# Four graph layers on one core: turning blocks by VectorE and DMAs in the second layer, and on two queues for the fourth

## The chip, the core and the metric

The kernel runs on one core of a Trainium2 chip, in one launch. Its time is the device time of the program in microseconds, from executions on the chip. A core has TensorE (PE in the profile), VectorE (DVE), ScalarE (ACT), GpSimd (POOL) and SyncE (SP). SP does no arithmetic and only issues DMAs; POOL computes and issues DMAs too. A queue is the order in which one engine issues its DMAs. Sixteen DMA engines carry them all.

## The reference

There are 4096 nodes with 256 features each and one 0/1 adjacency matrix. Four graph layers follow each other, and each ends in `x = layernorm(x + layer(x))`.

```python
# layer 0: additive attention, 4 heads, leaky_relu 0.2, masked softmax over j, elu
e = leaky_relu(s_i[:, None, :] + s_j[None, :, :], 0.2);  alpha = softmax(where(adj, e, -inf), axis=1)
# layer 1: dot-product attention, 4 heads of 64
q = x @ Wq + bq;  k = x @ Wk + bk;  v = x @ Wv + bv        # each split into 4 heads
scores = einsum('hnd,hmd->hnm', q, k) / 8 + (edge.T - 1) * 10000
ctx = einsum('hnm,hmd->hnd', softmax(scores), v)
# layer 2: additive attention, one head, slope 0.01, elu
# layer 3: cosine attention on features of width 128
att = softmax(where(adj > 0, normalise(x @ Wk.T) @ normalise(x @ Wq.T).T, NEG), axis=1)
out = 0.5 * (att @ x) + 0.5 * x
```

The text counts the layers from one: the second layer is the dot-product attention, the fourth is the cosine attention.

## The kernel before

All of it is float32. The features stay on the chip in `X`, 128 partitions by 32 tiles of 128 rows. A block is four tiles, 512 rows, so there are eight blocks (`NB = 8`, `QB = 4`, `QW = 512`). Every layer makes attention weights for one block of queries against one tile of keys at a time (a unit), always with the keys on the partitions, so that the product with the values needs no transpose of the weights. The weights of a unit are made on ScalarE (the exponential or a relu) and VectorE (the product with the mask), and TensorE sums over the keys into PSUM. The order of TensorE's work is written out by hand (`tc.manual_schedule`); in the second layer's attention those of VectorE and ScalarE are too. For the rest the framework's scheduler decides, and it moves an instruction ahead when it holds its inputs and its buffers to be there. Every engine issues in order, so an instruction that waits holds up what stands behind it on its engine or queue.

A projection of a block needs that block turned, with the features on the partitions. Two helpers do it. `transposed_block` (L112) lets TensorE do eight transposes of 128 x 128 (L118) into two PSUM banks, and two copies bring them to SBUF (L120). `turned_apart` (L123, called through `block_apart`, L138) does without TensorE: VectorE transposes 32 x 32 squares inside each quarter of the partitions (L130, two instructions of 128 x 512), one DMA writes the 512 KB result `squares` to DRAM (L133), and four DMAs of 128 KB read it back with the quarters exchanged (L135). The rows of the block come out in another order this way.

The second layer (`multi_head_attention`, L531) starts with a prologue. For each block TensorE turns it (`turn`, L564), multiplies it by Wk and Wq (`keys`, L567, matmuls L572, then ScalarE adds the bias at L576 and VectorE takes the largest magnitude at L577), and by Wv (`values`, L580, matmuls L587, additions L592 from two PSUM buffers `pv`). In the loop at L618 a pass turns block b, takes the values of block b - 1 and the keys of block b; block 0 was turned in the first layer. Then come 8 blocks of 64 half tiles of 64 keys: `scores` (L634) loads the mask, multiplies k and q of all four heads (L645) and lets ScalarE take the exponential (L647); `weights` (L649) multiplies by the mask on VectorE (L657) and adds up the row sums, on POOL (L664) for even half tiles and by an accumulating DMA from POOL's queue (L670) for odd ones, the first two of a block by plain DMAs from SP (L668); `sums` (L672) multiplies by V (L678). The weights `prob` have eight buffers. The mask is in bytes: during the first layer `narrow` (L946) copies the matrix from int32 to bytes in DRAM, in pieces `edges` of 64 rows by 16 half tiles by 512 columns, and `narrow_edges` gives four half tiles of one piece, so that each of two DMAs (L640) moves 64 partitions of 2 KB.

The third layer (`additive_one`, L401) has 8 blocks of 32 units: `weights` (L444: relu on ScalarE, L451; the mask on VectorE, L453) and `sums` (L455, four matmuls L459). The mask comes in int32 from SP, 512 KB for two units, into four buffers. During its last block the fourth layer is prepared by `Cosine.prepare` (L837), for blocks 0 to 5: step 0 turns X with `block_apart`; step 1 projects the block onto 128 features for queries and 128 for keys on TensorE (L852) and scales them to unit length as `rows`; step 2 turns `rows` with `turned_apart` into `T`. The calls stand at L513 and L521; one block follows another every four units, and step 1 stands eight units behind step 0. Both turnings go through POOL's queue, one buffer `squares` (pool `co_once`) and two in DRAM (`co_dram`). Blocks 6 and 7 are prepared in the fourth layer's first block, with both turnings on SP's queue. POOL's queue also carries the fourth layer's masks (L835), some of them behind a small copy that holds them back (`behind`, L91).

The fourth layer (`cosine_attention`, L868) has 8 blocks of 32 units again, with matmuls of `T` against `T` (L889) and of the weights against `X` (L901).

Of the kernel before, what the change touches and what calls it, by code (L numbers as in the profile page):

```python
# [9 lines left out]
FP = mybir.dt.float32  # L10
# [8 lines left out]
P = 128  # L19
# [9 lines left out]
def kernel(  # L29
# [92 lines left out]

    def turned_apart(once, dr, part, to, eng):  # L123

        B = P // QB
        squares = once.tile([P, QB, KC, P], FP, name="squares")
        for c in range(KC):
            nc.vector.transpose(squares[:, :, c, :].rearrange("p q (k n) -> p k q n", n=B),  # L130
                                part(c).rearrange("p k (q f) -> p k q f", f=B))
        far = dr.tile([QB, B, QB, KC * P], FP, name="squares_far")
        eng.dma_start(far.rearrange("a f q m -> (a f) (q m)"), squares.rearrange("p q c m -> p (q c m)"))  # L133
        for q in range(QB):
            eng.dma_start(to[q * B:(q + 1) * B], far[:, :, q, :].rearrange("a f m -> f a m"))  # L135
        return to.rearrange("p a (c m) -> p c a m", c=KC)
# [264 lines left out]
    def additive_one(w_sb, slope, tail, op, follow):  # L401
# [3 lines left out]
        with ExitStack() as lay:  # L405
# [18 lines left out]
            def turn(b):  # L424
                return transposed_block(sb, bank, b)

# [104 lines left out]
    def multi_head_attention(w_sb, b_sb, tail, rows_of_den, narrow_edges):  # L531
# [12 lines left out]
        with ExitStack() as lay:  # L544
# [7 lines left out]
            with ExitStack() as pro:  # L552
                wp = pool(pro, "mh_w", 1)
                sb = pool(pro, "mh_in", 3)
                ps = pool(pro, "mh_ps", 6, space=PSUM)
# [11 lines left out]
                def keys(b):  # L567
                    for n, to, scale in (("k", kT, 1.0), ("q", qT, qscale)):
                        for o in range(KC):
                            pk = bank()  # L570
                            for c in range(KC):
                                nc.tensor.matmul(pk, w_sb[n][:, c, o * P:(o + 1) * P],  # L572
                                                 xTs[b][:, c].rearrange("p k i -> p (k i)"),
                                                 start=(c == 0), stop=(c == KC - 1))
                            part = to[:, o, b * QW:(b + 1) * QW]
                            nc.scalar.activation(part, pk, AF.Identity, bias=b_sb[n][:, o:o + 1], scale=scale)  # L576
                            nc.vector.tensor_reduce(big[n][:, b, o:o + 1], part, AX.X, OP.max,  # L577
                                                    apply_absolute_value=True)

                def values(b):  # L580


                    for k in range(0, QB, KC):
                        pv = pv2.tile([P, KC, D], FP, name="pv")
                        for s in range(KC):
                            for c in range(KC):
                                nc.tensor.matmul(pv[:, s, :], xTs[b][:, c, k + s], w_sb["v"][:, c, :],  # L587
                                                 start=(c == 0), stop=(c == KC - 1))
                        j = 2 * (b * QB + k)
                        for n in range(2):  # L590
                            for r in range(2):
                                nc.vector.tensor_tensor(V[r * d:(r + 1) * d, j + n:j + n + 2 * KC - 1:2, :],  # L592
                                                        pv[n * d:(n + 1) * d, :, r * P:(r + 1) * P],
                                                        b_sb["v"][n * d:(n + 1) * d, r * P:(r + 1) * P].unsqueeze(1)
                                                        .to_broadcast([d, KC, P]), OP.add)
# [213 lines left out]
    class Cosine:  # L809
# [7 lines left out]
        def start(self):  # L817
# [5 lines left out]
            self.T = [keep.tile([P, QB, 2 * P], FP, name=f"T{b}") for b in range(NB)]  # L823
            self.dram = self.stack.enter_context(tc.tile_pool(name="co_dram", bufs=2, space=bass.MemoryType.DRAM))
            self.once = self.stack.enter_context(tc.tile_pool(name="co_once", bufs=1, side="right", reuse_waits="tile"))
            self.w_sb = keep.tile([P, KC, 2 * P], FP, name="w3_sb")
            load_w(self.w_sb[:, :, :P], wq3T, nc.sync)
# [116 lines left out]
    todo = iter([(b, j) for b in range(NB) for j in range(0, 2 * NT, NJ)])  # L944

    def narrow(z):  # L946

        for b, j in itertools.islice(todo, 1):
            slim_edges[b, j] = slim.tile([P // 2, NJ, QW], U8, name=f"edges{b}_{j}")
            with behind(z):  # L950
                nc.gpsimd.dma_start(slim_edges[b, j],
                                    adj.rearrange("(t p) i -> p t i", p=P // 2)[:, j:j + NJ, b * QW:(b + 1) * QW])

    def narrow_edges(b, j, n):
        return slim_edges[b, j - j % NJ][:, j % NJ:j % NJ + n, :]

# [70 lines left out]
```

## Time and profile before

| | |
|---|---|
| time | 2911.56 us, median of 3 runs (2909.53 to 2911.84) |
| profiled execution | 2912.43 us; 2910.7 us of it from first to last instruction |
| mean granted clock of TensorE | 0.997 |

| stretch, us from the start | what | PE busy, us | DVE | ACT | POOL | DMA share |
|---|---|---|---|---|---|---|
| 0 to 724 | first layer | 720.3 | 667.2 | 661.4 | 63.1 | 0.65 |
| 724 to 816 | second layer, prologue | 91.5 | 57.2 | 31.7 | 0.0 | 0.00 |
| 816 to 1717 | second layer, attention | 900.2 | 686.8 | 566.6 | 807.3 | 0.89 |
| 1717 to 2232 | third layer | 506.3 | 300.6 | 226.0 | 49.9 | 0.58 |
| 2232 to 2911 | fourth layer | 671.1 | 242.4 | 169.6 | 44.9 | 0.39 |

Busy time is the time in which an engine had an instruction at work. The DMA share is the mean busy share of the 16 DMA engines. PEld is TensorE's load of the stationary operand, which runs beside its matmuls. In the lines of the profile a group is named by its line in the kernel, its engine, its operation and `output<-input` in the program's names.

### The profile page before, as it was taken

Reading aid. Unit: us, or ns where it says so; the run is one execution under the profiler, and the core shown is the slowest. Engines: PE = TensorE matmul, PEld = TensorE weight load, DVE = VectorE, ACT = ScalarE, POOL = GpSimd, SP = SyncE. Lnnn points to the kernel's source line nnn. Section 1 sums busy time; section 2 is a strip of 40 time slices with the busy share of each in tenths; the row PEclk is TensorE's granted clock in tenths of the full one; section 3 lists DMA queues with packets and bytes.
Section 4 is the critical chain, followed back from the end, with each engine's and each line's share of the span. In section 5 each row is a group of like instructions: output and inputs, shape, how many; then the busy total and the mean of one; then the engine's idle time right before and its main releaser. Section 6 shows DMA issues by size and latency. Waiting matters only on the chain.

```text
span 2910.7 us, 50256 instructions
## 1 busy us (share of the span) xinstructions
PE 2889.4 (99%) x20141; PEld 1553.4 (53%) x20141; DVE 1954.2 (67%) x2541; ACT 1655.3 (57%) x2589; POOL 965.2 (33%) x735
## 2 busy tenths in 40 slices
PE   9999999999999999999999999999998999999998
PEld 4333333333643333333333358888887777777776
DVE  8899999998677777777777765655666423333333
ACT  7899999997356666666666654444443222222222
POOL 0010010100068989989889860000012000000000
PEclk9999999999999999999999999999999999999999
DMA  7566667665068989889889875655566434434341
GB/s 205 103 138 137 139 139 145 135 129 90 1 134 193 185 186 193 183 187 192 182 189 191 182 171 133 178 163 150 154 185 168 87 58 58 58 58 58 58 58 29
DMA packets 214061, 391.72 MB, mean 135 GB/s; under 512 B 16338, under 2 KB 94146, under 8 KB 212931
## 3 DMA queue, kind: packets, MB, share of 16 engines
q0 software_dynamic: 106336, 190.35, 40.2%
q1 hardware_dynamic: 107216, 197.88, 22.3%
q8 instruction: 158, 2.59, 0.3%
q14 instruction: 77, 0.62, 0.1%
q10 hardware_dynamic: 274, 0.26, 0.0%
HBM read 325.46 MB, written 29.43 MB: 122 GB/s over the span
## 4 chain that ended last, share of the span: by engine, by line
PE 98%; DMA 1%; DVE 1%; ACT 0%; issue 0%; POOL 0%; DVEq 0%; POOLq 0%
PE acc L293 23%; PE acc L901 15%; PE acc L678 15%; PE p L645 15%; PE acc L459 8%; PE g L459 7%; PE p L889 4%; PE g L889 3%; PE g L572 2%; PE g L196 1%; PE pv L587 1%; PE acc L196 1%; PE g L118 1%; PE acc L852 1%; DMA squares_far<-squares 1%; PE g L305 0%
## 5 line engine op out<-in xcount | busy, mean ns | idle before, releaser
L657 DVE TENSOR_TENSOR prob<-p,mask 128x1024 f32<-128x1024 f32 x512 | 624.1, 1223 | 209.5 <-ACT p L647 203.8
L647 ACT ACTIVATE p<-p,shift 128x1024 f32<-128x1024 f32 x512 | 556.2, 1088 | 325.2 <-PE p L645 324.4
L293 PE MATMUL acc<-prob,V 128*32 128x512 f32 x6144 | 664.0, 592 | 1.2 <-DVE prob L283 1.2
L664 POOL TENSOR_TENSOR den<-den,prob 128x1024 f32<-128x1024 f32 x248 | 626.9, 2528 | 72.6 <-DVE prob L657 64.7
L280 ACT ACTIVATE prob<-row,dst 128x512 f32<-128x512 f32 x1020 | 633.1, 712 | 0.1
L283 DVE SCALAR_TENSOR_TENSOR prob<-prob,mask 128x2048 f32<-128x2048 f32 x256 | 582.5, 2286 | 24.2 <-ACT prob L280 20.7
L645 PE MATMUL p<-qT,kT 64*64 64x512 f32 x4096 | 532.3, 590 | 0.8 <-DVE prob L657 0.8
L678 PE MATMUL acc<-prob,V 64*64 64x512 f32 x4096 | 531.5, 589 | 0.0
L901 PE MATMUL acc<-X,prob 128*128 128x257 f32 x2048 | 485.5, 380 | 0.0
L901 PEld LDWEIGHTS acc<-X,prob 128*128 128x128 f32 x2048 | 388.6, 190 | 162.8 <-issue 112.9
L894 DVE TENSOR_TENSOR prob<-prob,mask 128x512 f32<-128x512 f32 x256 | 176.2, 690 | 409.3 <-ACT prob L893 408.1
L293 PEld LDWEIGHTS acc<-prob,V 128*32 128x32 f32 x6144 | 197.3, 110 | 453.1 <-issue 433.6
L451 ACT ACTIVATE e<-row,dst 128x512 f32<-128x512 f32 x256 | 184.0, 721 | 241.8 <-DVE prob L453 212.6
L678 PEld LDWEIGHTS acc<-prob,V 64*64 64x64 f32 x4096 | 155.9, 133 | 285.4 <-issue 278.1
L645 PEld LDWEIGHTS p<-qT,kT 64*64 64x64 f32 x4096 | 154.4, 133 | 277.3 <-issue 261.5
L453 DVE SCALAR_TENSOR_TENSOR prob<-e,mask 128x512 f32<-128x512 f32 x256 | 177.6, 695 | 173.4 <-PE acc L459 93.9
L91 POOL COPY tick<-prob 128x1 f32<-128x1 f32 x35 | 40.0, 1144 | 645.9 <-DVE prob L283 644.8
L835 POOL DMA_DIRECT2D mask<-in_adjT x64 | 47.6, 743 | 582.2 <-DVE prob L894 505.3
L670 POOL DMA_DIRECT2D den<-prob x240 | 231.6, 965 | 14.7 <-DVE prob L657 7.5
L893 ACT ACTIVATE prob<-p 128x512 f32<-128x512 f32 x144 | 85.7, 596 | 257.0 <-PE p L889 243.0
L459 PE MATMUL acc<-V,prob 128*128 128x257 f32 x1024 | 225.1, 380 | 0.0
L459 PE MATMUL g<-V,prob 128*128 128x257 f32 x1024 | 224.1, 380 | 0.0
(160 smaller groups left out, 1965.6 us busy)
## 6 DMA issues: line engine op xcount, KB each, us to landing
mask<-in_adjT SPq DMA_DIRECT2D x256, 512.0 KB
den<-prob POOLq DMA_DIRECT2D x240, 512.0 KB, 5.3
mask<-edges SPq DMA_DIRECT2D x256, 128.0 KB
mask<-in_adjT POOLq DMA_DIRECT2D x64, 512.0 KB, 5.7
edges<-in_adj POOLq DMA_DIRECT2D x32, 512.0 KB, 10.0
den<-prob SPq DMA_DIRECT2D x16, 512.0 KB
row<-far SPq DMA_DIRECT2D x7, 1024.0 KB
squares_far<-squares POOLq DMA_DIRECT2D x12, 512.0 KB, 4.0
```

The source lines that it names most:

```text
L280: nc.scalar.activation(z[:, h, :], r, AF.Relu, bias=-1.0, scale=dst[:, j, h:h + 1])
L283: nc.vector.scalar_tensor_tensor(z, z, 1.0, mask[m][:, j % MJ, :].unsqueeze(1).to_broadcast([P, H, QW]), OP.add, OP.mult)
L293: nc.tensor.matmul(acc[b][h * G:(h + 1) * G, n, :], part, prob[b, j][:, h, :], start=(j == 0), stop=(j == NT - 1))
L459: nc.tensor.matmul(acc[b][k][:, :D + 1], prob[b, j][:, k * P:(k + 1) * P], V[:, j, :], start=(j == 0), stop=(j == NT - 1))
L645: nc.tensor.matmul(p[c * d:(c + 1) * d, r, :], kT[half, c, j * d:(j + 1) * d], qT[half, c, cols], start=True, stop=True)
L647: nc.scalar.activation(p, p, AF.Exp, bias=shift)
L657: nc.vector.tensor_tensor(z, p, mask[m][:, j % MJ, :].unsqueeze(1).to_broadcast([P, KC, QW]), OP.mult)
L664: nc.gpsimd.tensor_tensor(to, to, flat, OP.add)
L670: nc.gpsimd.dma_start(to, flat, accum_op=OP.add)
L678: nc.tensor.matmul(acc[b][c][r * d:(r + 1) * d, :], V[half, j, r * d:(r + 1) * d], prob[b, j][half, r, :], start=(j == 0), stop=(j == NH - 1))
L889: nc.tensor.matmul(p.rearrange("p (k i) -> p k i", k=QB), T[j // QB][:, 0, j % QB], T[b][:, 1], start=True, stop=True)
L901: nc.tensor.matmul(acc[b][k], prob[b, j][:, k * P:(k + 1) * P], X[:, j, :], start=(j == 0), stop=(j == NT - 1))
```

## The change

In the second layer, blocks 2 to 7 are turned by `block_apart` on SP's queue, one pass of the loop ahead of their use, with four xT buffers instead of three; block 1 is still turned by TensorE. The keys of these blocks then stand in the order in which the turning leaves them. The queries are put back in order as ScalarE writes them (L587 of the changed kernel), V is stored by the new order (L603), `scores` takes the keys from a column `at`, and the bytes of the mask are kept in pieces of 32 rows by 32 quarter tiles, from which four DMAs of 32 partitions fetch a mask tile, for the first 16 half tiles of a block in runs of 512 bytes. For the fourth layer step 0 has its own buffers (`follow.turning`: three xT buffers, which the third layer's own turnings use first, one `squares`, and DRAM) and goes to SP's queue; step 2 stays on POOL's for blocks 0 to 5. `rows` moves to the pool with one buffer.

```diff
-    def turned_apart(once, dr, part, to, eng):
+    def turned_apart(squares, far, part, to, eng):
-        squares = once.tile([P, QB, KC, P], FP, name="squares")
+        squares = squares.tile([P, QB, KC, P], FP, name="squares")
+        far = far.tile([QB, B, QB, KC * P], FP, name="far")
...
-        far = dr.tile([QB, B, QB, KC * P], FP, name="squares_far")
@@ additive_one
+            xp = pool(lay, "gb_turn", 3)
+            sq = pool(lay, "gb_squares", 1)
+            far = pool(lay, "gb_far", 2, space=bass.MemoryType.DRAM)
+            follow.turning = xp, sq, far
...
-                return transposed_block(sb, bank, b)
+                return transposed_block(xp, bank, b)
@@ multi_head_attention
-                sb = pool(pro, "mh_in", 3)
+                sb = pool(pro, "mh_in", 4)
+                sq = pool(pro, "mh_sq", 1)
+                dr = pool(pro, "mh_far", 2, space=bass.MemoryType.DRAM)
...
-                                nc.tensor.matmul(pk, w_sb[n][:, c, o * P:(o + 1) * P],
-                                                 xTs[b][:, c].rearrange("p k i -> p (k i)"),
+                                nc.tensor.matmul(pk.rearrange("p (k i) -> p k i", k=QB),
+                                                 w_sb[n][:, c, o * P:(o + 1) * P], xTs[b][:, c],
...
+                            if n == "q" and b > 1:
+                                part, pk = (t.rearrange(how, a=QB, n=P // QB) for t, how in
+                                            ((part, "p (k a n) -> p a k n"), (pk, "p (a k n) -> p a k n")))
...
+                    turn(1)
                     for b in range(1, NB):
-                        turn(b)
+                        if b < NB - 1:
+                            xTs[b + 1] = block_apart(sb, sq, dr, b + 1, nc.sync)
...
                     for c in range(KC):
-                        nc.sync.dma_start(mask[m][c * d:(c + 1) * d], narrow_edges(b, j, MJ))
+                        for s in range(2):
+                            lo = c * d + s * d // 2
+                            nc.sync.dma_start(mask[m][lo:lo + d // 2], narrow_edges(b, j, s))
...
+                at = j * d if j < 4 * QB else j // (2 * QB) * QW + j % QB * P + j % (2 * QB) // QB * d
...
-                        nc.tensor.matmul(p[c * d:(c + 1) * d, r, :], kT[half, c, j * d:(j + 1) * d], qT[half, c, cols],
+                        nc.tensor.matmul(p[c * d:(c + 1) * d, r, :], kT[half, c, at:at + d], qT[half, c, cols],
@@ Cosine.prepare
-            eng = nc.gpsimd if b < NB - 2 else nc.sync
             if step == 0:
-                self.xT[b] = block_apart(in_, self.once, self.dram, b, eng)
+                self.xT[b] = block_apart(*self.turning, b, nc.sync)
...
-                rows = self.rows[b] = in_.tile([P, QB, 2, P], FP, name="rows")
+                rows = self.rows[b] = self.once.tile([P, QB, 2, P], FP, name="rows")
...
-                turned_apart(self.once, self.dram, lambda n: rows[:, :, n, :], self.T[b], eng)
+                turned_apart(self.once, self.far, lambda n: rows[:, :, n, :], self.T[b],
+                             nc.gpsimd if b < NB - 2 else nc.sync)
@@ cosine_attention
+            co.turning = (pool(lay, "co_turn", 2), pool(lay, "co_squares", 1),
+                          pool(lay, "co_turn_far", 2, space=bass.MemoryType.DRAM))
@@ narrow, narrow_edges
-    NJ = 16
+    NJ = 32
...
-            slim_edges[b, j] = slim.tile([P // 2, NJ, QW], U8, name=f"edges{b}_{j}")
+            slim_edges[b, j] = slim.tile([P // QB, NJ, QW], U8, name=f"edges{b}_{j}")
...
-    def narrow_edges(b, j, n):
-        return slim_edges[b, j - j % NJ][:, j % NJ:j % NJ + n, :]
+    def narrow_edges(b, j, s):
+        t = 2 * j
+        part = slim_edges[b, t - t % NJ]
+        if j < 4 * QB:
+            return part[:, t + s:t + s + 2 * QB - 1:2, :]
+        t = t % NJ // (QB * QB) * QB * QB + (j % (2 * QB) // QB * 2 + s) * QB
+        return part[:, t:t + QB, :]
```

More of the change, by code (lines that the diff above doesn't have):

```diff
@@ L571, in keys @@
                             for c in range(KC):
[L572 to L573 removed]
+                                nc.tensor.matmul(pk.rearrange("p (k i) -> p k i", k=QB),
+                                                 w_sb[n][:, c, o * P:(o + 1) * P], xTs[b][:, c],
                                                  start=(c == 0), stop=(c == KC - 1))
                             part = to[:, o, b * QW:(b + 1) * QW]
+                            if n == "q" and b > 1:
+                                part, pk = (t.rearrange(how, a=QB, n=P // QB) for t, how in
+                                            ((part, "p (k a n) -> p a k n"), (pk, "p (a k n) -> p a k n")))
                             nc.scalar.activation(part, pk, AF.Identity, bias=b_sb[n][:, o:o + 1], scale=scale)
[L577 removed]
+                            nc.vector.tensor_reduce(big[n][:, b, o:o + 1], to[:, o, b * QW:(b + 1) * QW], AX.X, OP.max,
                                                     apply_absolute_value=True)
@@ L588, in values @@
                                                  start=(c == 0), stop=(c == KC - 1))
-                        j = 2 * (b * QB + k)
                         for n in range(2):
+                            j = slice(None, KC) if b > 1 else slice(None, 2 * KC - 1, 2)
+                            first = 2 * b * QB + (n * QB + k if b > 1 else 2 * k + n)
+                            j = slice(first, first + j.stop, j.step)
                             for r in range(2):
-                                nc.vector.tensor_tensor(V[r * d:(r + 1) * d, j + n:j + n + 2 * KC - 1:2, :],
+                                nc.vector.tensor_tensor(V[r * d:(r + 1) * d, j, :],
                                                         pv[n * d:(n + 1) * d, :, r * P:(r + 1) * P],
@@ L823, in start @@
             self.T = [keep.tile([P, QB, 2 * P], FP, name=f"T{b}") for b in range(NB)]
-            self.dram = self.stack.enter_context(tc.tile_pool(name="co_dram", bufs=2, space=bass.MemoryType.DRAM))
             self.once = self.stack.enter_context(tc.tile_pool(name="co_once", bufs=1, side="right", reuse_waits="tile"))
+            self.far = self.stack.enter_context(tc.tile_pool(name="co_far", bufs=2, space=bass.MemoryType.DRAM))
             self.w_sb = keep.tile([P, KC, 2 * P], FP, name="w3_sb")
@@ L938, in cosine_attention @@
                         outputs(b, QB if b < NB - 1 else 2)
-    NJ = 16
+    NJ = 32
     slim = ctx.enter_context(tc.tile_pool(name="slim", bufs=1, space=bass.MemoryType.DRAM))
     slim_edges = {}
-    todo = iter([(b, j) for b in range(NB) for j in range(0, 2 * NT, NJ)])
+    todo = iter([(b, j) for b in range(NB) for j in range(0, QB * NT, NJ)])
     def narrow(z):
         for b, j in itertools.islice(todo, 1):
-            slim_edges[b, j] = slim.tile([P // 2, NJ, QW], U8, name=f"edges{b}_{j}")
+            slim_edges[b, j] = slim.tile([P // QB, NJ, QW], U8, name=f"edges{b}_{j}")
             with behind(z):
                 nc.gpsimd.dma_start(slim_edges[b, j],
-                                    adj.rearrange("(t p) i -> p t i", p=P // 2)[:, j:j + NJ, b * QW:(b + 1) * QW])
-    def narrow_edges(b, j, n):
-        return slim_edges[b, j - j % NJ][:, j % NJ:j % NJ + n, :]
+                                    adj.rearrange("(t p) i -> p t i", p=P // QB)[:, j:j + NJ, b * QW:(b + 1) * QW])
+    def narrow_edges(b, j, s):
[5 more added lines that the diff above has]
+        return part[:, t:t + QB, :]
     w2_sb = const.tile([P, KC, D + 2], FP, name="w2_sb")
```

## The prediction

> **What bounds the kernel now.** I read the page first, then PE's waits, then the places they name.
>
> ```profile
> PE 2889.4 (99%) x20141; PEld 1553.4 (53%) x20141; DVE 1954.2 (67%) x2541; ACT 1655.3 (57%) x2589; POOL 965.2 (33%) x735
> ...
> PE 98%; DMA 1%; DVE 1%; ACT 0%; issue 0%; POOL 0%; DVEq 0%; POOLq 0%
> ```
>
> TensorE is the bound, and 98% of the chain is its work. Time can come only from PE work taken away or from the 1% in which it waits. The waits of PE name one that is large (columns: total us, times, longest):
>
> ```profile
> PE acc L852 <- DMA xT<-squares_far: 8.7, 2, 7.9
> ```
>
> The timeline of PE there, at the end of the third layer, where blocks are projected for the fourth:
>
> ```profile
> 2169.93 3.62 PE L852 MATMUL acc<-w_sb,xT 128*128 128x256 f32 x16
> ...
> 2181.28 3.69 PE L852 MATMUL acc<-w_sb,xT 128*128 128x256 f32 x16 [0.79 <-DMA xT<-squares_far]
> 2184.81 7.10 PE L459 MATMUL g<-V,prob 128*128 128x257 f32 x32
> 2199.81 6.55 PE L852 MATMUL acc<-w_sb,xT 128*128 128x256 f32 x16 [7.90 <-DMA xT<-squares_far]
> ```
>
> After a wait of 0.79 us sixteen matmuls took their usual time; after 7.90 us they took 6.55, about 3.0 more than 3.6 (chain: 6.55 against 3.45, so 3.1). The windows answer gives a granted clock of 0.53 for 2200 to 2206. The stall costs 0.79 + 7.90 + 3.1 = 11.8 us. Why xT is late is in POOL's timeline:
>
> ```profile
> 2175.23 0.56 POOL L133 DMA_DIRECT2D squares_far<-squares  x1 [0.86 <-DVE squares L130]
> ...
> 2183.00 2.20 POOL L135 DMA_DIRECT2D T<-squares_far  x4 [4.71 <-DMA squares_far<-squares]
> 2185.20 0.57 POOL L133 DMA_DIRECT2D squares_far<-squares  x1
> 2194.33 2.18 POOL L135 DMA_DIRECT2D xT<-squares_far  x4 [8.56 <-DMA squares_far<-squares]
> ```
>
> One queue and one `squares` buffer carry two turnings per block in turn: a T write landing after 7.2 us, its reads, an X write landing after 8.6, then the xT reads PE waits for. A block's projection and its four units take about 10.4 us of PE (four times 1.74, and 3.45), so two turnings don't fit.
>
> The second layer's prologue, PE's timeline:
>
> ```profile
> 755.54 1.04 PE L118 MATMUL g<-ident,X 128*128 128x128 f32 x8
> 756.41 3.62 PE L587 MATMUL pv<-wv_sb,xT 128*128 128x256 f32 x16
> 759.87 3.60 PE L572 MATMUL g<-xT,wk_sb 128*128 128x512 f32 x8
> 763.30 3.60 PE L572 MATMUL g<-xT,wq_sb 128*128 128x512 f32 x8
> 766.74 1.04 PE L118 MATMUL g<-ident,X 128*128 128x128 f32 x8
> ```
>
> PE runs without a gap. From the start of the transposes to the next matmuls, eight of them cost 756.41 - 755.54 = 0.87 us of each 11.20 us block. The stages around:
>
> ```profile
> 768.00:779.00 11.00, 11.00 (x40) 6.74 (x40) 5.93 (x13) 3.52 (x7) 0.00 (x0) 1.00 0.00 0
> ...
> 820.00:848.00 28.00, 28.00 (x264) 10.05 (x268) 20.48 (x18) 17.99 (x17) 24.41 (x15) 1.00 0.77 180
> ...
> 876.00:904.00 28.00, 28.00 (x264) 9.95 (x260) 20.13 (x17) 17.94 (x17) 26.09 (x17) 1.00 0.96 195
> ```
>
> (PE, PEld, DVE, ACT, POOL busy, clock, DMA share, GB/s.) In the prologue DVE, ACT and the DMA engines have room; in the attention that follows POOL and DMA are nearly full.
>
> **The change, part by part.**
>
> *Six blocks turned without PE.* 48 transposes go: 6 x 0.87 = 5.2 us, all on PE's path. With them goes a wait of 0.38 us at 801.74, where the last block's projection stood directly behind its own turning (`ACT xT L120`). ACT loses 12 copies of 0.59 us. DVE gains 12 transposes of 0.70 us (L130's median): 1.4 us a block, 5.9 becomes 7.3 of about 10.3 us, hidden. SP gains 6 writes of 512 KB and 24 reads of 128 KB. They stand behind the first 12 mask loads and before the first two den loads, which need scores at 800 or later, so nothing urgent is behind them. In the trace SP's first masks issue from 698 to 716; twelve at 0.6 us are through by 720.
>
> Is each xT in time? On an idle SP a write took 2.7 us to its reads (2237.58 to 2240.29); four reads take 2.2 us to issue and about 3 to land. Block 2: squares at 726, read by 737, wanted at 748 (724.5 + keys 6.9 + tail and one turning 2.5 + values 3.5 + keys 6.9 + values 3.5). Block 4 is the tightest: DVE's order puts the second half of its transposes behind the values of block 1, about 754; write 754.5, reads 757 to 759, landed by 762, wanted at 768.5. Blocks 5 to 7 have 12 us or more. `squares` has one buffer, so DVE stands at a transpose until the write before has landed; behind it wait the maximum reductions and additions to V. PE would feel that through two pv buffers: the worst, at 757, leaves values(2) added by 762.5, when PE wants the buffer at 765. Cost 0; if the cover went, a late xT would cost its lateness, plus about 3 us of clock if it is long (somewhere between 0.79 and 7.90 us).
>
> The keys' matmuls now stream four pieces of 128 columns. L889 streams T in such pieces and has 592 ns in the line groups, as L572 has: no cost. ACT writes q in runs of 32, for which the trace has no row: between the 0.69 us it takes now and twice that (a guess at a bad case, 1.4 us more per block on an engine under 4 of 10 us busy), hidden either way.
>
> *Half tiles and byte masks in the resulting order.* The matmuls, exponentials and multiplications of the attention stay the same in number and shape. 256 mask loads of 128 KB (64 partitions, 2 KB runs) become 512 of 64 KB; for the first 16 of each block's 64 half tiles the runs are 512 bytes. SP issues them at 0.59 us: 4 per 6.9 us, 2.4 us, not its bound. The DMA engines are another matter:
>
> ```profile
> q1 hardware_dynamic: 879, 1.44, 11.8%
> ...
> q1 hardware_dynamic: 5785, 6.74, 93.2%
> ```
>
> The first is 860 to 900: about 703 mask packets of 2 KB carry its 11.8% x 40 us x 16, so 107 ns each, or 128 x 107 / 16 = 0.86 us per mask tile. The second is the first 22 us, mostly X in 1 KB packets: 57 ns on average. No row has a 512-byte load on this queue; I bound it by half of 57 (28 ns) below and 57 above. A tile of 512 packets then costs 0.9 to 1.8 us, up to +0.96 in 6.9 us, for four tiles of a block's sixteen. At the start of a block the share is only 0.77, since the first den tiles are plain loads. To reach the 0.96 seen later, 28 us have 5 us free, against 4 x 0.96 = 3.9. I take 28 and cost 0. The Trainium skill speaks against it: "DMA: Bandwidth & Descriptors", section Bandwidth, has transfers under 64 KB descriptor-dominated and 0.95 us for one of 64 KB. Read as engine time, four would be 3.8 us per tile instead of 0.86, the share would pass 1 all stage long, and 0.3 of 894 us would be lost. But this trace's loads, at twice the size, cost 0.43 us each with a den accumulation beside them: that page times a transfer standing alone, and here many overlap. I go by the row.
>
> The narrowing keeps 32 DMAs of 1024 rows each.
>
> *Turning for the fourth layer.* POOL loses 6 writes and 24 reads of 0.56 us each and SP gains them: in the built order step 0 goes to SP with its own squares and xT buffers (three instead of two). All six X transposes and writes, and the reads of blocks 0 to 2, now stand far back in the third layer, between mask loads; DVE there is at 58%. Reads for blocks 3, 4, 5 stand behind mask loads whose buffers come free at units 5, 9 and 13 of the last block, each just after the projection that frees an xT buffer. So xT 3 is issued near 2157 (times of before), lands by 2162 and is wanted near 2180; 4 and 5 have some 20 us too. Masks behind these reads have eight units (14 us) of lead. POOL keeps one turning per block: write 4 to 8.6 us,
>
> ```profile
> DMA to landing us min/median/max: 2.9/4.0/8.6
> ```
>
> then 2.2 us of issue: 6.2 to 10.8 against 10.4. T is wanted only in the fourth layer. All 11.8 us go. For blocks 6 and 7 SP's new order puts X write and reads of 7 before T's write of 6; in the trace X 7 is normalised at 2246, so its reads are out by 2252, before T 6 is ready (2259). No cost. `rows` with one buffer is rewritten only after its transposes, on the same engine.
>
> Sum: 5.2 + 0.4 + 11.8 = 17.4 us. The profiled execution was 2912.4 us (span 2910.7), 0.9 above the median 2911.56; it becomes 2895.0, the median 2894.2.
>
> **Rivals.**
> 1. *The DMA engines, not the queue, were full.* Their share from 2169 to 2200 reads 1.02 to 1.03, and mask loads for both layers are still there. If writes keep landing after 8.6 us, DVE, in order, stands at T's transposes; PE has about two units (3.4 us) in hand. Against: the X writes leave the stretch. Half the stall stays, or the prologue's tightest xT is some us late: 6 lost, 2900.
> 2. *Slower: 512-byte packets make DMA the bound of the second layer.* Narrowing's packets (26014 on POOL's queue in 140 to 690, 29.8%, so 101 ns) end as 512 bytes. At 101 ns a tile costs 3.2 us, four cost 9.5 more than now, 4.5 beyond the free 5; prob buffers come back late, and 8 blocks lose 36 us: 2930. It outweighs the gain from 2.2 us a block, near 77 ns. Against: those packets read 2 KB and cast.
> 3. *A turn misplaced:* SP, in order, holds a mask behind a read and gives most of the gain back: 2908, the same.
>
> **Numbers.** Forecast 0.76 (2891 to 2897); rival 1 0.13; rival 2 0.08, of which milder forms end inside no change; rival 3 0.03. No change is within 0.2% (5.8 us), about what runs of this kernel can tell. Faster 0.88, same 0.05, slower 0.07. The range 2891 to 2901 holds the forecast and most of rival 1.
>
> **What would show it.** Right: no PE wait on an xT DMA, no clock below 1 near 2200, 48 transposes fewer at L118, a block period of 10.33 in the prologue, the second layer's attention still near 901 us. Wrong: PE waiting at keys or values; PE or DVE waiting on den accumulations; DMA share at 1 early in each block.

## The result, and the profile after

| | before | after |
|---|---|---|
| time | 2911.70 us, median of 4 runs (2909.53 to 2913.19) | 2893.18 us, median of 4 runs (2892.71 to 2893.66) |
| profiled execution | 2912.43 us, span 2910.7 | 2893.66 us, span 2891.9 |

The ratio is 0.9937, 95% interval 0.9922 to 0.9952: 18.5 us are gone. The forecast was 2894.2, and 17.4 us. The page of the changed kernel (busy time, share of the span and instructions of each engine, then the shares of the chain):

```profile
PE 2879.8 (100%) x20093; PEld 1546.5 (53%) x20093; DVE 1960.4 (68%) x2553; ACT 1649.3 (57%) x2577; POOL 946.7 (33%) x705
...
PE 99%; DVE 0%; ACT 0%; DMA 0%; issue 0%; SPq 0%; DVEq 0%; ACTq 0%
```

TensorE has 48 instructions and 9.6 us less. DMA, with 1% of the chain before, has less than half a percent. PE's longest waits (us in total, times, longest); none names an xT DMA any more:

```profile
PE acc L293 <- DVE prob L283: 1.2, 1, 1.2
PE acc L358 <- DVE ones L73: 1.1, 1, 1.1
PE p L664 <- DVE prob L676: 0.8, 1, 0.8
```

PE's timeline at the end of the third layer, the place of the 7.90 us:

```profile
2173.43 3.62 PE L869 MATMUL acc<-w_sb,xT 128*128 128x256 f32 x16
2176.88 7.10 PE L464 MATMUL g<-V,prob 128*128 128x257 f32 x32
2183.82 3.62 PE L869 MATMUL acc<-w_sb,xT 128*128 128x256 f32 x16
...
2194.21 3.62 PE L869 MATMUL acc<-w_sb,xT 128*128 128x256 f32 x16
```

Every projection (L869) takes 3.62 us, they follow each other every 10.39 us, and the granted clock from 2200 to 2206 is 1.00 (0.53 before). POOL's timeline there shows that step 2, which stayed on its queue, can still be slow:

```profile
2162.97 0.56 POOL L133 DMA_DIRECT2D far<-squares  x1 [0.77 <-DVE squares L131]
...
2172.04 2.20 POOL L135 DMA_DIRECT2D T<-far  x4 [8.51 <-DMA far<-squares]
2183.99 0.56 POOL L133 DMA_DIRECT2D far<-squares  x1 [1.17 <-DVE squares L131]
...
2193.02 2.18 POOL L135 DMA_DIRECT2D T<-far  x4 [8.46 <-DMA far<-squares]
```

POOL still waits up to 8.5 us for a write of `squares` to land, for two of these blocks; for the others 2.9 to 4.9. The DMA share from 2160 to 2200 is 1.00 (0.98 before), as full as it was. But no xT stands behind these writes now: SP's timeline has the reads of xT at

```profile
2145.91 2.68 SPq L135 DMA_DIRECT2D xT<-far  x4
2156.30 1.92 SPq L135 DMA_DIRECT2D xT<-far  x4
2166.68 2.22 SPq L135 DMA_DIRECT2D xT<-far  x4
```

each issued some 27 us ahead of its projection (blocks 3, 4 and 5: 2173.43, 2183.82, 2194.21). The prologue of the second layer, PE:

```profile
754.11 3.62 PE L598 MATMUL pv<-wv_sb,xT 128*128 128x256 f32 x16
757.56 3.60 PE L579 MATMUL g<-xT,wk_sb 128*128 128x512 f32 x8
760.99 3.60 PE L579 MATMUL g<-xT,wq_sb 128*128 128x512 f32 x8
764.43 3.62 PE L598 MATMUL pv<-wv_sb,xT 128*128 128x256 f32 x16
```

The transposes (L118) between `values` and `keys` are gone, and a block takes 764.43 - 754.11 = 10.32 us. The second layer's attention, in windows (PE, PEld, DVE, ACT, POOL busy, clock, DMA share, GB/s):

```profile
811.00:839.00 28.00, 27.19 (x256) 9.54 (x252) 21.43 (x20) 18.71 (x18) 22.25 (x14) 1.00 0.70 160
...
810.00:1711.00 901.00, 900.15 (x8392) 320.79 (x8389) 686.99 (x672) 566.93 (x548) 806.09 (x523) 1.00 0.90 186
```

901 us for the stage, as before. Early in a block, in the place of 820 to 848 before (813.5 to 841.5 here), the DMA share is 0.79 against 0.77. Where the 18.8 us of span went, by the starts of the same instructions in the two traces: 5.90 in the prologue (first keys to first scores, 91.81 to 85.91), 12.23 in the stretch of the six projections (first L852 to 2232.20 before, 83.25; first L869 to 2213.28 after, 71.02), 0.56 ahead of the first layer's sums (before, PE waited 0.58 us for the DMA of `a_row`; nothing of the change stands there), 0.2 in between, and -0.1 at the end.

### The profile page after: what moved, and what is told of

Its sections match the earlier page's. It is cut to its first block, busy times and chain, and to the rows that moved or that the text cites. A ratio compares the mean times of both kernels' runs of the same rounds, so it can differ in the third digit from the quotient of the medians.

```text
span 2891.9 us, 50575 instructions
## 1 busy us (share of the span) xinstructions
PE 2879.8 (100%) x20093; PEld 1546.5 (53%) x20093; DVE 1960.4 (68%) x2553; ACT 1649.3 (57%) x2577; POOL 946.7 (33%) x705
## 4 chain that ended last, share of the span: by engine, by line
PE 99%; DVE 0%; ACT 0%; DMA 0%; issue 0%; SPq 0%; DVEq 0%; ACTq 0%
PE acc L293 23%; PE p L664 15%; PE acc L922 15%; PE acc L697 15%; PE acc L464 8%; PE g L464 8%; PE p L910 4%; PE g L910 3%; PE g L579 2%; PE g L196 1%; PE pv L598 1%; PE acc L869 1%; PE acc L196 1%; PE g L118 1%; PE g L305 0%; PE p L734 0%
```

## The experiments

Each was timed beside the kernel before, on the same chip; ratios are to it. Its medians in these series were 2911.6 to 2912.4.

**The two halves alone.** `e1_second_alone` has the second layer's part, with step 0 for the fourth layer as before:

```diff
...
-                self.xT[b] = block_apart(*self.turning, b, nc.sync)
+                self.xT[b] = block_apart(in_, self.once, self.far, b, nc.gpsimd if b < NB - 2 else nc.sync)
...
-                rows = self.rows[b] = self.once.tile([P, QB, 2, P], FP, name="rows")
+                rows = self.rows[b] = in_.tile([P, QB, 2, P], FP, name="rows")
...
```

> The second layer's part alone; the fourth layer is turned as before. Theory (two gains that add up: PE work taken out of the prologue, and a queue that no longer runs late): the prologue shrinks as in the changed kernel, 5.9 us from the first keys to the first scores, and the stall near 2190 stays with its slow clock, 12 us: 2905.8 us. Rival (the DMAs of the prologue or the smaller mask loads cost the attention something that the other part hides): an attention longer than 901 us, or a time above 2907.

`e2_fourth_alone` has the fourth layer's part, with the second layer as before:

```diff
...
-                    turn(1)
                     for b in range(1, NB):
-                        if b < NB - 1:
-                            xTs[b + 1] = block_apart(sb, sq, dr, b + 1, nc.sync)
+                        turn(b)
...
-    NJ = 32
+    NJ = 16
...
```

> The fourth layer's part alone; the second layer with PE's transposes and two mask loads per tile as before. Theory: no wait of PE on an xT DMA, the prologue as before (91.8 us): 2911.7 - 12.2 = 2899.5 us. Rival (the third layer gained because the second left the DMA queues earlier or in another order): part of the stall comes back, above 2902.

Measured: 2905.72 us (2903.54 to 2906.97), ratio 0.9977, interval 0.9968 to 0.9986, for the first; 2899.57 (2899.07 to 2901.66), 0.9957, 0.9945 to 0.9970, for the second. Against the median of before in that series, 2912.05, these are 6.3 and 12.5 us, and 6.3 + 12.5 = 18.8: within the runs' scatter the halves add up. The timeline of PE in the first still has the stall:

```profile
2173.96 3.69 PE L864 MATMUL acc<-w_sb,xT 128*128 128x256 f32 x16 [1.22 <-DMA xT<-far]
...
2192.56 5.22 PE L864 MATMUL acc<-w_sb,xT 128*128 128x256 f32 x16 [7.96 <-DMA xT<-far]
```

and PE's waits in the second have no xT DMA, but still the small one of the prologue:

```profile
PE g L577 <- ACT xT L120: 0.4, 1, 0.4
```

**Queue or buffer?** The change gives the X turning another queue and other buffers at once. `e3_own_pool` keeps the buffers and goes back to POOL's queue:

```diff
-                self.xT[b] = block_apart(*self.turning, b, nc.sync)
+                self.xT[b] = block_apart(*self.turning, b, nc.gpsimd if b < NB - 2 else nc.sync)
```

> The changed kernel, but step 0 of blocks 0 to 5 back on POOL's queue, its own squares and three xT buffers kept. If one queue was what made xT late: POOL needs a write's landing (8.5 us) and two times 2.2 us of issue per block, 13 against 10.4, three times; xT has some 20 us in hand, T's transposes have not, and the stall returns in part, 2896 to 2903. If the shared buffer was: the X writes are early as in the changed kernel and the time stays at 2893.

`e4_shared_sp` keeps SP's queue and goes back to the old buffers for `squares`, xT, `rows` and DRAM:

```diff
...
-                self.xT[b] = block_apart(*self.turning, b, nc.sync)
+                self.xT[b] = block_apart(in_, self.once, self.far, b, nc.sync)
...
```

> The changed kernel, but step 0 with the buffers of before (squares shared with step 2, two xT buffers), on SP's queue. If one queue was what made xT late: no stall, 2893. If the shared buffer was: X and T transposes still take turns behind each other's landed writes, 3 us on SP and up to 8.5 on POOL per block, 11.5 and more against 10.4, and a stall of 3 to 12 us stays: 2896 to 2905.

Measured: e3 2894.25 us (2893.43 to 2895.51), ratio 0.9939, 0.9926 to 0.9951; e4 2902.20 (2901.29 to 2904.54), 0.9967, 0.9954 to 0.9979. `e1_second_alone` is the kernel with neither, at 2905.72. From there the second queue alone brings 3.5 us, the buffers alone 11.5, and both 12.5: with the buffers there, the queue adds about 1 us, within the runs' scatter, and with the queue there, the buffers add 9. With one queue but its own buffers the X writes and the xT reads of blocks 0 to 2 stand far back in the third layer too: VectorE's X transposes of e3 lie between 1818.7 and 2097.5, those of the changed kernel between 1819.8 and 2098.6. Only delays of some 0.3 us for each of three blocks are left in e3.

e4 goes back on several things at once, so two more runs part `squares` from the number of xT buffers. `e7_shared_squares` shares `squares` and DRAM buffers but has three xT buffers; `e8_two_xt` has its own `squares` and two xT buffers:

```diff
# e7_shared_squares
-                self.xT[b] = block_apart(*self.turning, b, nc.sync)
+                self.xT[b] = block_apart(self.turning[0], self.once, self.far, b, nc.sync)
# e8_two_xt
-            xp = pool(lay, "gb_turn", 3)
+            xp = pool(lay, "gb_turn", 2)
```

> The changed kernel, but step 0 for the fourth layer uses the buffer `squares` and the DRAM buffers of step 2 again; it keeps SP's queue and three xT buffers. If the shared `squares` alone made xT late (VectorE stands at a transpose until the other turning's write has landed), this is near e4_shared_sp: 2901 to 2903, PE waiting several us at the fourth layer's projections or at the third layer's units. If it was the number of xT buffers, this is near the changed kernel, 2893 to 2894, with no PE wait over 1 us there. Both in part: in between, 2896 to 2899.

> The changed kernel with two xT buffers for step 0 instead of three; `squares` stays its own. VectorE's order is that of the changed kernel, and only SP's reads of xT move behind masks. If the own `squares` does the work, 2893 to 2894 and no PE wait on xT. If the third xT buffer does, the reads come too late for a projection: 2896 to 2902 and a PE wait on the xT DMA of one block or more.

Measured: e7 2901.80 us (2900.67 to 2902.41), ratio 0.9965, 0.9952 to 0.9977: all of e4's loss. e8 2894.88 (2892.69 to 2895.57), 0.9940, 0.9928 to 0.9953, its span 2892.1: near the changed kernel. It is `squares`: the wait that costs e7 its time stands on VectorE, which writes `squares` and never the DRAM buffers. VectorE's timeline in e7 shows how:

```profile
2168.21 0.69 DVE L875 COPY rows<-acc 128x512 f32<-128x512 f32 x1 [1.82 <-ACT sq L874]
2172.88 1.30 DVE L131 STREAM_TRANSPOSE squares<-X 128x512 f32<-128x512 f32 x2 [3.98 <-DMA far<-squares]
2174.11 0.65 DVE L875 COPY rows<-acc 128x512 f32<-128x512 f32 x1
2174.68 0.15 DVE L877 TENSOR_SCALAR v<-norm 128x8 f32<-128x8 f32 x1
2174.75 0.68 DVE L458 SCALAR_TENSOR_TENSOR prob<-e,mask 128x512 f32<-128x512 f32 x1
```

and PE's in e7 who pays:

```profile
2166.78 5.37 PE L464 MATMUL g<-V,prob 128*128 128x257 f32 x24
2175.48 3.79 PE L464 MATMUL g<-V,prob 128*128 128x257 f32 x8 [3.33 <-DVE prob L458]
2179.07 4.58 PE L869 MATMUL acc<-w_sb,xT 128*128 128x256 f32 x16
```

The X transposes of a later block stand 3.98 us at the head of VectorE, until the other turning's write (on POOL at 2165.50, its reads at 2173.14 after 7.08 us) has left `squares`. Behind them stands the multiplication that makes the next weights, at 2174.75, and PE waits 3.33 us for it. In the old kernel the same buffer made xT itself late. VectorE's timeline there:

```profile
2182.45 1.30 DVE L130 STREAM_TRANSPOSE squares<-X 128x512 f32<-128x512 f32 x2 [1.15 <-DMA squares_far<-squares]
...
2200.61 1.30 DVE L130 STREAM_TRANSPOSE squares<-X 128x512 f32<-128x512 f32 x2 [5.50 <-DMA squares_far<-squares]
```

The X transposes of block 4 begin at 2182.45, when the T write of 2175.23 has left `squares`. They end at 2183.75, and their write goes out at 2185.20, behind T's reads on POOL: 1.45 us for the queue. The rest is the T write's landing (7.2 us), the X write's own (8.6) and the reads. With its own `squares` the X transposes wait for nothing but the X writes before them, and the scheduler places them far ahead: the X writes of blocks 3 to 5 go out at 1988, 2044 and 2099, against 2168, 2185 and 2203 before. No run keeps an own `squares` but leaves these writes in the stretch where the DMA engines are full, so how much is the buffer as such and how much the earlier place that it allows is not shown.

**The price of the clock.** The prediction counted 3.1 us for matmuls that ran slowly after the 7.90 us wait. After nearly the same wait in e1, 7.96 us, the sixteen matmuls took 5.22 us, so the price was 1.6 there. `e6_filler` and `e10_filler_half` are the kernel before, with matmuls put ahead of the projection of block 4, so that PE is at work in the wait; their results are overwritten:

```diff
-                    pr = bank().rearrange("p (t n f) -> p t n f", t=2, f=P)
+                    raw = bank()
+                    for _ in range(64 if (b, k) == (4, 0) else 0):       # 32 in e10_filler_half
+                        nc.tensor.matmul(raw[:, :P], ones, ones, start=True, stop=True)
+                    pr = raw.rearrange("p (t n f) -> p t n f", t=2, f=P)
```

> The kernel before, with 64 matmuls of ones (128 columns each, about 7 us, results overwritten) put directly ahead of the fourth layer's projection of block 4, where PE waited 7.9 us. The wait for xT stays as long; only PE is at work in it. If the 3.1 us by which the sixteen matmuls behind the wait were slow came from PE's standing still, they are back near 3.6 us, and the time is 2911.7 - 3 = 2908.5 to 2909. If they were slow for another reason, the time is 2911.5 to 2912 as before; if the filler delays the projection, above 2912.

> e6_filler with 32 matmuls of ones instead of 64. In e6_filler the 64 took 14.45 us and not 7, so they outlasted the wait. Half take 7.2 us, less than the wait of 7.9. If standing still costs the clock, the sixteen matmuls behind take 3.6 us, and the time is 3 us under the kernel before: 2908.6 (PE waits about 0.7 us for xT). If not, they take 6.5 us again: 2911.6.

Measured: e6 2915.33 us (2913.26 to 2918.57), ratio 1.0013, 1.0007 to 1.0020. The filler was sized wrongly: 14.45 us, twice what the transposes' rows had suggested. It took the place of 7.9 + 3.1 = 11.0 us, and the span grew by 3.5 (2914.2). Behind it the sixteen matmuls took 3.62 us. e10: 2916.15 (2913.62 to 2918.49), ratio 1.0013, 1.0007 to 1.0020; not faster, against the expectation. Its profiled execution, at the low end with 2914.29, shows in PE's timeline why:

```profile
2190.67 7.31 PE L851 MATMUL acc<-ones 128*128 128x128 f32 x64
2198.95 3.69 PE L855 MATMUL acc<-w_sb,xT 128*128 128x256 f32 x16 [0.97 <-DMA xT<-squares_far]
2202.48 7.10 PE L459 MATMUL g<-V,prob 128*128 128x257 f32 x32
2213.28 5.38 PE L855 MATMUL acc<-w_sb,xT 128*128 128x256 f32 x16 [3.70 <-DMA xT<-squares_far]
```

The mechanism is right: with PE at work the matmuls of block 4 take 3.69 us at a granted clock of 1.00 (2199 to 2202.6), not 6.55 at 0.53. But the 3 us come back at once. Block 5's xT is late too, PE waits 3.70 us for it, and its projection starts at 2213.28, against 2213.13 before, and it is now the one that runs slowly, at 0.67. In this execution the slow clock of the old kernel had only hidden that the turnings were late for the next block as well. Why the median lies 3 to 4 us above that of before, while the profiled span is 1.8 above, stays open.

**Shorter mask packets.** The second rival rested on the cost of a 512-byte packet, which no row of before showed, in a quarter of the tiles. `e5_runs512` and `e5_runs256` are the changed kernel with all mask loads of the second layer in such runs, and in runs of half the length:

```diff
# e5_runs512
-            slim_edges[b, j] = slim.tile([P // QB, NJ, QW], U8, name=f"edges{b}_{j}")
+            slim_edges[b, j] = slim.tile([P // QB, NJ, 2 * QW], U8, name=f"edges{b}_{j}")
...
# e5_runs256
+            slim_edges[b, j] = slim.tile([P // QB, NJ, 2, QW], U8, name=f"edges{b}_{j}")
...
+                rows = adj.rearrange("(t p) i -> p t i", p=P // QB)[:, j:j + NJ, :]
+                for c in range(2):
+                    lo = b * QW + c * 256
+                    nc.gpsimd.dma_start(slim_edges[b, j][:, :, c, :256], rows[:, :, lo:lo + 256])
...
```

> The changed kernel with byte pieces of the mask whose rows stand 1024 bytes apart, so that all mask loads of the second layer move runs of 512 bytes, not only the first quarter of each block: four times the disputed packets. At 28 us per thousand packets over 16 engines (28 ns a packet) a mask tile costs 0.90 us as before: 2893 to 2894, DMA share in the second layer 0.90. At 57 ns a tile costs 1.8 us, about 1 us in 6.9 us more, the share goes from 0.90 to 1 and the stage begins to wait: 2900 to 2930. At 77 ns or more it is slower than the kernel before.

> The changed kernel with all mask loads of the second layer in runs of 256 bytes: bytes kept in column halves of rows 1024 bytes apart, two narrowing DMAs a piece, and eight instead of four loads for a mask tile in the first quarter of each block. If a packet's cost goes with its bytes (2 KB 103 ns, 512 bytes 28 ns), 256 bytes cost 14 ns: no change, 2893 to 2894. If 28 ns is near the least that a packet takes, a tile costs 1.8 us instead of 0.9, the share of 0.96 late in a block goes past 1: the second layer's attention takes 901 us plus up to 60, 2900 to 2950, with PE waiting on prob buffers that den accumulations hold.

Measured: 2893.18 us (2892.55 to 2894.66), ratio 0.9937, 0.9924 to 0.9949, and 2893.40 (2892.86 to 2894.65), 0.9937, 0.9923 to 0.9950. Neither is slower than the changed kernel. The DMA view for 860 to 900 (queue, packets, MB, share of 16 engines), the changed kernel first,

```profile
q1 hardware_dynamic: 1082, 1.46, 12.6%
```

then e5_runs512,

```profile
q1 hardware_dynamic: 3264, 1.48, 14.3%
```

and e5_runs256:

```profile
q1 hardware_dynamic: 6013, 1.45, 16.8%
```

The packets' time is the share x 40 us x 16: 91.5 us for 3264 packets, 28 ns each, and 107.5 us for 6013, 18 ns each. By the megabytes some 350 to 370 of each count are shorter packets; if these cost nothing, a mask packet takes 32 and 19 ns. Four times the mask packets cost 1.7 points of the share. Over the whole stage the share of all queues goes from 0.90 to 0.91 and 0.94, and PE's busy time stays 900.15 of 901 us. From 860 to 900 it goes from 0.95 to 0.96 and 1.00, so with 256 bytes no room is left there. The expectation for 256 bytes had a floor near 28 ns or half of it; the packet lies between, and PE does not feel it.

**More blocks without PE.** If a turning by VectorE and DMAs is free, more of them should be a gain. `e9_more_apart` turns block 1 of the second layer that way, and blocks 4 to 7 of the third, there with two copies (VectorE and ScalarE) that put the columns back in order. `e12_four_more` leaves block 7 to PE and has two `squares` buffers in the third layer, and two xT buffers:

```diff
# e9_more_apart
...
+                    xTs[1] = block_apart(sb, sq, dr, 1, nc.sync)
                     keys(0)
                     tail(bank)
-                    turn(1)
...
+            def natural(xT):
+                to = nat.tile([P, KC, QB, P], FP, name="nat")
+                for c, copy in enumerate((nc.vector.tensor_copy, nc.scalar.copy)):
+                    copy(to[:, c].rearrange("p k (a n) -> p a k n", n=P // QB),
+                         xT[:, c].rearrange("p a (k n) -> p a k n", n=P // QB))
+                return to
...
-                                xTs[n] = turn(n)
+                                if n < 4:
+                                    xTs[n] = turn(n)
+                                if n + 2 < NB:
+                                    m = n + 2
+                                    xTs[m] = natural(block_apart(xp, sq, far, m, nc.sync))
...
# e12_four_more, against e9_more_apart
-                                if n < 4:
+                                if n < 4 or n == NB - 1:
...
-                                if n + 2 < NB:
+                                if n + 2 < NB - 1:
...
-            sq = pool(lay, "gb_squares", 1)
+            sq = pool(lay, "gb_squares", 2)
-            xp = pool(lay, "gb_turn", 3)
+            xp = pool(lay, "gb_turn", 2)
```

> The changed kernel with five more blocks turned without PE: block 1 of the second layer, and blocks 4 to 7 of the third layer, there with two copies on VectorE and ScalarE that put the columns back in order. If every xT is in time, PE's work falls by 5 x 0.87 = 4.35 us: 2888.8. If the reads land late behind the third layer's masks on SP, PE waits at the projections of that layer and most is given back: 2892 to 2900. If VectorE's transposes hold up the weights of the third layer's first block: above 2893.

> e9_more_apart without its late block: block 7 of the third layer is turned by PE again, blocks 4, 5 and 6 stay apart, and the third layer's `squares` has two buffers (xT two instead of three to make room). In e9_more_apart the copies of block 7 stood 16 us on VectorE and ScalarE for the reads, with the weights behind them, and PE lost 9.3 us and some clock. Without it PE's work falls by 4 x 0.87 = 3.5 us against the changed kernel and nothing waits over 2 us: 2889.5 to 2891.5, below both kernels. If the three writes at the start of the third layer collide with its first masks, VectorE stands there again: 2893 or more.

Measured: e9 2904.30 us (2894.32 to 2906.18), ratio 0.9969, 0.9958 to 0.9981: 11 us slower than the changed kernel in the median, though one of the six runs came to 2894.32. VectorE's timeline,

```profile
1781.36 0.43 DVE L436 COPY nat<-xT 128x512 f32<-128x512 f32 x1 [16.16 <-DMA xT<-far]
1781.70 1.29 DVE L466 SCALAR_TENSOR_TENSOR prob<-e,mask 128x512 f32<-128x512 f32 x2
```

and PE's:

```profile
1769.51 3.65 PE L196 MATMUL g<-w_sb,nat 128*128 128x258 f32 x16
1782.44 8.81 PE L472 MATMUL acc<-V,prob 128*128 128x257 f32 x32 [9.28 <-DVE prob L466]
```

Block 7's write went out at 1756.38 and its reads at 1769.32, 13 us later, with the third layer's masks in the same stretch (DMA share 0.69 from 1756 to 1770 and 0.78 from 1750 to 1783; in the changed kernel 0.53 from 1750 to 1783). The copy had been placed ahead of the next weights and stood 16 us at the head of VectorE. e12: 2892.81 us (2891.56 to 2899.60), ratio 0.9941, 0.9928 to 0.9955. That can't be told from the changed kernel's 2893.18. PE has 3.5 us less work (2876.3 against 2879.8), but at the start of the third layer it waits once more:

```profile
1722.13 2.00 PE L472 MATMUL acc<-V,prob 128*128 128x257 f32 x8 [2.46 <-DVE prob L466]
```

The transposes of three blocks now stand ahead of the first weights on VectorE. So 3.5 us less work and 2.5 us more waiting leave a span 0.9 us shorter (2891.0 against 2891.9), and the 2889.5 to 2891.5 us that were expected did not come. No version here is shown to beat the changed kernel.

## Why the prediction was right, point by point

*The sum: 17.4 us predicted, 18.5 measured.* 0.56 us of the profiled executions' difference lies at `a_row` and is no part of the change: that wait varies among the other runs too (0.3 us in e3, 0.6 in e9).

*Transposes: 5.2 + 0.38 us predicted, 5.90 measured.* 48 instructions went from L118 (19.0 us busy after, 25.0 before, with those that stay), and the period is the predicted one. What was missed is small: at 801.74 the old kernel needed 1.42 us from the transposes to the keys, 0.55 more than 0.87, of which the wait named in the prediction is 0.38. e1 alone gives 6.3 on its medians.

*Each xT in time: right.* Block 4, the tightest, was written at 754.04 (754.5 predicted) and read from 756.82; the second layer's `values` and `keys` never wait. VectorE stood at `squares` as predicted, 4.5 us in two waits (2.93 ahead of 730.26 and 1.59 ahead of 756.77), hidden. ScalarE's q in runs of 32 takes 0.69 us, the lower end of its bounds, and the keys' matmuls in four pieces 3.60 us for eight, as before: both costs are zero, as taken.

*Mask packets: 28 ns taken, 28 to 32 ns measured (e5_runs512).* That the figures meet so closely is luck: 28 was half of 57, the lower end of a range that was called a bound. The second rival needed 77 by the prediction, 83 by its own figures: 0.86 + (5 + 2.2) / 4 = 2.66 us for a tile of 512 packets. It is out: four times as many of the packets change nothing. The rule weighed against this, in the Trainium skill, "DMA: Bandwidth & Descriptors", section Bandwidth, which has transfers under 64 KB descriptor-dominated and 0.95 us for one of 64 KB, would have filled the stage (of 901 us, not 894) if read as engine time. The page's 0.95 us is one load issued by GpSimd; the loads here are SP's. Here a 64 KB load of 512-byte packets takes 128 x 28 / 16 = 0.22 us of the sixteen engines, and with 256-byte packets 256 x 18 / 16 = 0.29. The measurement decides: for these loads, of which many overlap, the row in the trace was the right source.

*The stall: 11.8 us predicted, 12.23 measured; e2 alone 12.5.* Size right, and the wait on xT is gone. Two steps behind it have to be put more narrowly. First, "One queue and one `squares` buffer carry two turnings per block in turn": that the two turnings don't fit is right, but the weight is on the buffer. With two queues and one buffer 9 us of the gain are lost (e4, e7); with one queue and two buffers about 1 (e3). The title, and the prediction's account by POOL's order of issue, put the weight on the queue. POOL's waits of 4.71 and 8.56 us between issues are landings of the writes that the next reads fetch. They can't tell queue from buffer, since the next transposes wait for the same landings; VectorE's lines and e3 and e4 can. Second, the 3.1 us of slow clock are one execution's price (1.6 in e1), and they were not to be had alone. e10 shows this for the kernel before: the next xT came at the same time whatever PE did, and the gain turned into a wait of 3.70 us. The sum was right because the change removed the lateness of every block together.

*First rival, full DMA engines: half true and without effect.* POOL still waits up to 8.5 us for T's writes, with the share at 1.00. The prediction had VectorE then stand at T's transposes; it stands 0.2 us in all at `squares` between 1780 and 2215, since the next T transposes come 10.4 us later. e7 is what that rival looks like when it does act.

*Third rival, a turn misplaced on SP:* did not occur in the changed kernel (27 us in hand, where the prediction had about 20). e9 is its near relative: an instruction that waits for a turn put ahead of the weights, on VectorE instead of SP, for 9.28 us and the slow matmuls after it.

## What to carry to other kernels

When two streams of work share an engine in order and a staging buffer, count the time until the DMA out of the buffer lands, not the time to issue it. If two such landings don't fit in a period, try a second buffer before a second queue: here it brought 11.5 us alone, the queue 3.5. A free engine and a free DMA queue are not enough to move work off the bound engine for nothing: what waits for the landing stands somewhere in order, and must not stand ahead of what feeds the bound engine. A stall that is taken out must be followed to the next user of the same resource, for it may only have hidden that one's lateness.

## What the runs showed of the hardware

The cost of a mask packet fell with its length, but less than in proportion: 107 ns for 2 KB (the kernel before), 32 for 512 bytes, 19 for 256, with the queue's whole time put on the mask packets; spread over all its packets it is 86, 28 and 18. The same 512 KB write took 2.8 us from issue to the next reads with no other transfer beside it (754.04 to 756.82), and 5.3 to 9.0 us with the DMA share at 1.00 (2195.20 to 2200.46, 2162.97 to 2172.04). In e9 it took 13 us at a share of 0.69, which in the last 5 us was only 0.23, so the share alone does not give it; what held that write is open.

How much a wait of PE cost in clock did not follow its length. Waits of up to 2.46 us cost 0.1 us at most (e12: eight matmuls in 2.00 us instead of 1.90). Waits of 3.23 and 3.33 us cost 3.0 and 2.9 (e4, e7), 3.70 us cost 1.8 (e10), 7.90 us 3.0 (the kernel before), 7.96 us 1.6 (e1) and 9.28 us 1.7 (e9: 8.81 us instead of 7.10 for 32 matmuls). Behind each of these the granted clock fell to 0.50, and it was back at 1.00 some 3 to 6 us after the wait. Why 3 in one case and 6 in another, these runs don't show. With PE at work in the wait, on results that nobody used, it cost nothing (sixteen matmuls in 3.62 us in e6 and 3.69 in e10). The same stationary and moving size, 128 by 128, cost 0.109 us as a transpose and 0.226 us as a matmul of ones (14.45 us for 64, which the trace counts as 128 instructions).
